# Side work in later slots, in_proj's input two blocks ahead, and three or four parts of the last image under way at once

## The chip, the core and the metric

The kernel runs on one core of one Trainium2 chip. The metric is device time in microseconds (us) from the start of the program to its end; the time of a kernel is the median of its runs. Inside the core five engines have an instruction queue each: TensorE (PE in the profile, with its weight loads as PEld), VectorE (DVE), ScalarE (ACT), GpSimd (POOL) and SyncE (SP), which here only issues DMAs. An engine takes its instructions in order; one that waits for a semaphore holds up all that stand behind it.

## The reference: what is computed

Four images of 64 x 64 positions with 96 channels go through four layers:

- **Layer 0**: a group normalization, then a state-space block: `in_proj` to a value half and a gate half, a depthwise 3x3 convolution with SiLU, and a selective scan in four directions (rows, columns, and both reversed). A step of the scan is `hst = hst * dA + (dl * ul) * B`, the output `y = sum over 16 states of hst * C`. The four directions are merged, normalized, multiplied by the gate and projected back to 96 channels; the input is added.
- **Layer 1**: the same kind of block on the real 2-D Fourier transform of each image (64 x 33 frequencies, 192 channels in), then the inverse transform, added to its input.
- **Layers 2 and 3**: a linear attention over the 4096 tokens of an image (done with a 97 x 97 Gram matrix), and a feed-forward layer of width 384 in fp8 (float8e5), each with a normalization before it and an addition to the token tensor after it.

```
h = h * dA + dt[..., None] * Bt[:, :, None, :] * ut[..., None]
y = jnp.einsum('bkdn,bkn->bkd', h, Ct)
```

## The kernel before, in words

**Three stretches.** The *head* (`begin`, to about 221 us) does the normalization and `project` of the first image pair alone. The *scan loop* (`scans`, L473 to L821) then runs six phases: layer 0 for two image pairs, layer 1 for four images. The *tail* (`end1` of image 3, after 11454 us) finishes the last image alone.

**The scan loop.** It has 1728 steps (L756), one for each segment of up to 512 positions, each quarter of the 16 states and each of three channel chunks. A step is written out in a fixed order (manual schedule, L713), so each engine's queue is exactly the order of the source. VectorE does per step: `hx` scan 0, `hx` scan 1, *slot 1*, `hy` scan 0, *slot 2*, `hy` scan 1, *slot 3*, and the product `hcy` (L781 to L815; the scans' line is L653). TensorE transposes the next step's input (`transposed`, L623) between slots 1 and 2 and accumulates the output (`accumulate`, L675) before and after slot 3. GpSimd forms `hy` (L646) and `hcx` (L798), ScalarE the exponentials (L628) and the scaled inputs `bx` (L593).

**Side work.** All else is cut into pieces by Python generators: a generator yields where its next piece may stand in another slot. `slot` (L733) first lets a piece of the next segment's `prepare` go, then adds `rate / 3` to `due` and takes one side piece when `due` reaches 1:

```
due = min(due + st.z.ph.rate / 3, 3.0)
if due >= 1.0:
    due -= E.step(kind)
```

`RATES` (L26) gives pieces per step for the six phases. A piece marked `LATE` only goes into slot 3, where VectorE's side work is cheap to place; `E.defer(fn)` queues an instruction (a PSUM eviction, an addition) that is issued at the beginning of the next piece, or of the next slot that is held. `E.psum` in the loop hands out one PSUM bank, so a piece's first matmul follows the last reader of the bank. The side tasks of phases 0 to 5 are, in this order: `flip0`, `begin0` of the second pair, two `gate0`; `end0` of a pair and `begin1` of two images (phases 1 and 2); `end1` of images 0, 1, 2 (phases 3, 4, 5). `E.require` (L770) would drain the queue outside the slots if a phase's input were late, and `E.finish` (L821) drains what is left after the last step.

**Places that the change touches.** `visits` (L184): in_proj's input `xi` is loaded one block ahead into two buffers, two yields before the first matmul (L176). `gated` (L350): per block of up to 8 rows, tiles of two rows are loaded (`yt`, `ut`, L364), added up on TensorE (`py`, L394 and L400), and normalized: mean `pm` (L414), subtraction on VectorE (L417), square (L420), variance `pv` (L424), then L431, L436 and the output projection. `out0` (L878) adds the projection `po` to `xr` on VectorE (L901); `out1` (L907) writes `att`. `inverse` (L990): three groups of 32 channels, one after the other: `piv` (L1021), `pio` (L1037), addition (L1040), write. `tokens` (L1049): per layer the eight weight tensors, then `layer_norm` (four parts of 8 tiles, pipelined over its own steps), the Gram matrix `pg` (L1136) and a chain of four small matmuls, eight groups of attention (`pt` L1157, copy `xt` L1159, `pao` L1163, addition L1165), a second `layer_norm`, eight groups of feed-forward (`ptf` L1172, cast `x8` L1174, `ph` L1180, copies L1181, VectorE L1184 and L1187, `pfo` L1192, copy L1200, additions L1202 and L1206), and at the end one store of the whole image (L1207).

In the head and the tail a side task runs alone with 8 PSUM banks and `wide=4`; no manual schedule holds there, and Tile's scheduler orders each queue. In the head, `project` already runs its three chunks through `together`, which takes one piece of each of several generators in turn (L111).

Of the kernel before, what the change touches and what calls it, by code (L numbers as in the profile page):

```python
# [6 lines left out]
F32 = mybir.dt.float32  # L7
# [14 lines left out]
C, P = 3, 128  # L22
# [3 lines left out]
RATES = [1.75, 2.25, 2.35, 2.35, 2.35, 2.35]  # L26
# [97 lines left out]
class Block:  # L124
# [59 lines left out]
    def visits(self, E, sp, wi, xf, blocks, half, nm, w, done):  # L184


        def load(r, n):
            x = sp.tile([CH, 2, 512], F32, name=f"xi{half}_{nm}_{r}", tag=f"xin{w}", bufs=2)
            self.nc.sync.dma_start(out=x[:, :, : n * 64], in_=xf[:, :, r * 64 : (r + n) * 64])
            return x  # L190

        nxt = load(*blocks[0])
        yield
        yield
        for b, (r, n) in enumerate(blocks):
            x, nxt = nxt, load(*blocks[b + 1]) if b + 1 < len(blocks) else None
            pi = E.psum(f"pi{half}_{nm}_{r}")
            yield from self.in_proj(pi, wi, half, x, n * 64)
            E.defer(lambda r=r, n=n, pi=pi: done(r, n, pi))
            yield  # L200
# [149 lines left out]
    def gated(self, E, g, io, out_proj):  # L350


        nc, cfg = self.nc, self.cfg
        yn, yo = io["y"][cfg.nat], io["y"][1 - cfg.nat].rearrange("k (w r) c -> r w k c", r=cfg.NR)
        u, gz = io["u"][cfg.nat], io["gz"]
        with E.pool(f"{cfg.pre}nm{g}") as sp:
# [3 lines left out]
            tiles = [  # L360
                (b, i, r + i, min(2, n - i)) for b, (r, n) in enumerate(cfg.rows) for i in range(0, n, 2)
            ]

            def load(b, i, r, n):  # L364
                nm = f"{cfg.pre}_{g}_{r}"
                yt = sp.tile([P, 2, 2, C * P], F32, name=f"yt_{nm}", tag="yt", bufs=2)
# [5 lines left out]
                ut = sp.tile([P, C, P], F32, name=f"ut_{nm}", tag="ut", bufs=2)  # L372
                nc.sync.dma_start(out=ut[:, :, : n * 64], in_=u[:, :, r * 64 : (r + n) * 64])
                return yt, ut

            todo = iter(tiles)
            nxt = load(*next(todo))
            yield
            yield
            yield  # L380
            for b, (r, nr) in enumerate(cfg.rows):
                n = nr * 64
                nm = f"{cfg.pre}_{g}_{r}"
                z = sp.tile([P, C, 512], F32, name=f"zb_{nm}", tag="zb")
                nc.sync.dma_start(out=z[:, :, :n], in_=gz[:, :, r * 64 : r * 64 + n])
                y = sp.tile([P, C, 512], F32, name=f"yb_{nm}", tag="yb")
                for i in range(0, nr, 2):
                    m = min(2, nr - i) * 64
                    yt, ut = nxt
                    more = next(todo, None)  # L390
                    nxt = load(*more) if more else None
                    ps = E.psum(f"py_{nm}_{i}")[:, : C * P].rearrange("p (c t) -> p c t", c=C)
                    for c in range(C):
                        nc.tensor.matmul(  # L394
                            ps[:, c, :m], self.skip[:, c, :], ut[:, c, :m], start=(c == 0), stop=False
                        )
                    yield
                    for c in range(C):
                        for k in range(4):
                            nc.tensor.matmul(  # L400
                                ps[:, c, :m],
                                yt[:m, k // 2, k % 2, c * P : (c + 1) * P],
                                self.ident[:m, :m],
                                start=False,
                                stop=(c == C - 1 and k == 3),
                                is_transpose=True,
                            )
                        if c < C - 1:
                            yield
                    E.defer(lambda i=i, m=m, ps=ps, y=y: nc.scalar.copy(y[:, :, i * 64 : i * 64 + m], ps[:, :, :m]))  # L410
                    yield
                pm = E.psum(f"pm_{nm}")
                for c in range(C):
                    nc.tensor.matmul(pm[:, :n], self.mean_w, y[:, c, :n], start=(c == 0), stop=(c == C - 1))  # L414
                    yield
                for c in range(C):
                    nc.vector.tensor_tensor(y[:, c, :n], y[:, c, :n], pm[:, :n], ALU.subtract)  # L417
                yield
                sq = sp.tile([P, C, 512], F32, name=f"sq_{nm}", tag="sq")
                nc.scalar.activation(sq[:, :, :n], y[:, :, :n], AF.Square)  # L420
                yield
                pv = E.psum(f"pv_{nm}")
                for c in range(C):
                    nc.tensor.matmul(pv[:, :n], self.mean_w, sq[:, c, :n], start=(c == 0), stop=(c == C - 1))  # L424
                    yield
                ln = sp.tile([P, 512], F32, name=f"ln_{nm}", tag="ln")
                nc.scalar.activation(ln[:, :n], pv[:, :n], AF.Ln, bias=self.eps)
                nc.scalar.activation(pv[:, :n], ln[:, :n], AF.Exp, scale=-0.5)
                yield
                for c in range(C):  # L430
                    nc.vector.scalar_tensor_tensor(  # L431
                        y[:, c, :n], y[:, c, :n], self.lnw[:, c : c + 1], pv[:, :n], ALU.mult, ALU.mult
                    )
                yield LATE
                for c in range(C):
                    nc.vector.scalar_tensor_tensor(  # L436
                        y[:, c, :n], y[:, c, :n], self.lnb[:, c : c + 1], z[:, c, :n], ALU.add, ALU.mult
                    )
                yield
                yield from out_proj(E, sp, wo, y, r, nr)  # L440
# [437 lines left out]
def out0(images, ins, x0):  # L878


    def task(E, blk, sp, wo, y, r, nr):
# [3 lines left out]
        for i, b in enumerate(images):  # L885
# [4 lines left out]
            for m in range(4):  # L890
# [8 lines left out]
                if m % 2:  # L899
                    yield  # L900
            nc.vector.tensor_tensor(xr, xr, po, ALU.add)  # L901
# [5 lines left out]
def out1(att, b):  # L907


    def task(E, blk, sp, wo, y, r, nr):  # L910
        nc = E.nc
        a = sp.tile([HH, 8, 2 * CH], F32, name=f"ab_{b}_{r}", tag="ab")
# [77 lines left out]
def inverse(E, cst, att, x, b, x1):  # L990
# [3 lines left out]
    G, HC, WP = 32, 16, 64  # L994
    xs, xd = (t.rearrange("(h w) c -> w h c", w=WW) for t in (x, x1))
    with E.pool(f"fi{b}") as sp:
# [5 lines left out]
        def load(c0):  # L1002
            a = sp.tile([2 * HH, WP, G], F32, name=f"at_{b}_{c0}", tag="at", bufs=2)
# [7 lines left out]
        nxt = load(0)  # L1011
        yield
        yield
        for c0 in range(0, CH, G):
            a, nxt = nxt, load(c0 + G) if c0 + G < CH else None
            v = sp.tile([2 * WP, G, HH], F32, name=f"v_{b}_{c0}", tag="v")
# [11 lines left out]
            for h0 in range(0, HH, 2 * HC):  # L1028
                xr = sp.tile([2 * WW, HC, G], F32, name=f"xr1_{b}_{c0}_{h0}", tag="xr", bufs=2)
# [11 lines left out]
                for p, h in halves:  # L1041
                    nc.sync.dma_start(out=xd[:, h, c0 : c0 + G], in_=xr[p])
        yield
# [5 lines left out]
def tokens(E, ins, consts, ident, x1, b, out):  # L1049


    nc = E.nc
    A = CH + 1
    with E.pool(f"tk{b}") as sp:
# [3 lines left out]
        nc.sync.dma_start(out=mask, in_=consts["head_mask"])  # L1058
        x = sp.tile([P, NT, CH], F32, name=f"tok_{b}", tag="tok")
        nc.sync.dma_start(out=x, in_=x1.rearrange("(p t) c -> p t c", t=NT))  # L1060
        xn = sp.tile([P, NT, A], F32, name=f"xn_{b}", tag="xn")
        nc.gpsimd.memset(xn[:, :, CH:A], 1.0)
        yield
        yield

        def layer_norm(nm):

            Q = 8
# [8 lines left out]
            for i in range(n + 2):  # L1077
# [3 lines left out]
                if i < n:  # L1081
                    t0 = i * Q
                    s = sp.tile([P, 2, Q], F32, name=f"lns_{nm}_{t0}", tag="lns", bufs=3)
# [13 lines left out]
                if i < n:  # L1097
                    sq = sp.tile([P, Q, CH], F32, name=f"lnq_{nm}_{t0}", tag="lnq", bufs=2)
                    nc.scalar.activation(sq, xq, AF.Square)
# [5 lines left out]

        def small(rows, lhs, rhs, name, into):
# [4 lines left out]

        for ly in (2, 3):
            nm = f"{b}_{ly}"
            wq = sp.tile([A, 3 * CH], F32, name=f"wqkv_{nm}", tag="wqkv")
            nc.sync.dma_start(out=wq, in_=ins[f"l{ly}_wqkv"])
            wqt = sp.tile([CH, A], F32, name=f"wqt_{nm}", tag="wqt")
            nc.sync.dma_start(out=wqt, in_=ins[f"l{ly}_wqt"])
            wff = sp.tile([CH, CH], F32, name=f"wff_{nm}", tag="wff")
            nc.sync.dma_start(out=wff, in_=ins[f"l{ly}_wff"])
            bff = sp.tile([A, CH], F32, name=f"bff_{nm}", tag="bff")  # L1120
            nc.sync.dma_start(out=bff, in_=ins[f"l{ly}_bff"])
            q = {}
            for name, shape in (("w1", [CH, 4 * CH]), ("w2", [P, 3, CH]), ("b1", [P, 3]), ("b2", [P, CH])):
                t = sp.tile(shape, F32, name=f"{name}_{nm}", tag=name)
                src = ins[f"l{ly}_{name}"]
                nc.sync.dma_start(out=t, in_=src.to_broadcast([P, CH]) if name == "b2" else src)
                q[name] = sp.tile(shape, F8, name=f"q{name}_{nm}", tag=f"q{name}")
                yield LATE
# [281 lines left out]
```

## Time and profile before

| what | value |
|---|---|
| median of 3 runs (lowest to highest) | 11915.16 us (11897.1 to 11918.08) |
| the profiled execution, own time | 11917.7 us |
| its span (first to last instruction) | 11915.9 us |
| granted TensorE clock over the span | 0.880 |
| VectorE busy in the loop, 300 to 11455 us | 10230.52 of 11155 us |
| TensorE busy there | 8885.92 us |
| first scan starts, last scan ends | 220.8 us, 11453.6 us |
| last image's gated block, 11458 to 11646 us | TensorE busy 120.52 of 188 us |
| last image's inverse transform, 11646 to 11694 us | TensorE busy 35.10 of 48 us |
| last image's two token layers, to the end | from about 11694 us |

The profiled execution took 11917.7 us, 1.8 us more than its span and 2.5 us more than the median. A row of groups reads: line, engine, operation, tiles, count, busy time, mean duration, and the idle time of that engine just before it with what ended it. A row of waits reads: who waited, for whom, total us, times, longest. A row of stretches gives the busy time of each engine in a window of the span, then the granted TensorE clock (1 is full speed), the DMA engines' mean busy share, and GB/s.

### The profile page before, as it was taken

The page shows a single profiled execution, that of the slowest core. Times are in us where ns is not written, and L with a number is a line of the kernel's source. Part 1 is how long each engine was busy: PE and PEld are TensorE (multiplying, and loading weights), DVE is VectorE, ACT ScalarE, POOL GpSimd, SP SyncE. Part 2 cuts the span into 40 slices and gives each one's busy share as a digit, 9 for nine tenths or more (in the row PEclk, how much of TensorE's full clock was granted, in tenths as well). Part 3 has the DMA queues.
Part 4 walks back from the last instruction along what each step waited for, and adds up shares of the span by engine and source line. Part 5 has one row for each costly group of instructions (what it writes and reads, how often), then busy time and mean ns, then how long its engine had stood idle before and what let it go on. Part 6 is the DMA issues. An engine that isn't in the chain of part 4 may idle for free. (4 is left out here: it accounts for less than half of the span.)

```text
span 11915.9 us, 164932 instructions
## 1 busy us (share of the span) xinstructions
PE 9346.5 (78%) x54800; PEld 6707.9 (56%) x54800; DVE 10559.1 (89%) x10183; ACT 9087.2 (76%) x18534; POOL 8930.4 (75%) x7074
## 2 busy tenths in 40 slices
PE   6678777787788778777888888788778877887765
PEld 3455555555666556556665565565556555565544
DVE  6899999999998999998889988988989899899954
ACT  3678888898777888887768877777777777777733
POOL 2889999888877898987668878877668766686630
PEclk8789989989888989998889989898889888897886
DMA  5454444556555455455543443544234422442231
GB/s 142 119 139 119 121 125 112 141 161 161 148 145 118 124 132 136 126 133 162 149 123 118 132 127 113 155 134 117 82 96 149 112 90 85 143 129 88 83 106 35
DMA packets 1270448, 1469.07 MB, mean 123 GB/s; under 512 B 496024, under 2 KB 1033824, under 8 KB 1260120
## 3 DMA queue, kind: packets, MB, share of 16 engines
q1 hardware_dynamic: 1269591, 1458.53, 44.5%
q8 instruction: 430, 7.05, 0.3%
q14 instruction: 427, 3.49, 0.1%
HBM read 1221.74 MB, written 236.50 MB: 122 GB/s over the span
## 5 line engine op out<-in xcount | busy, mean ns | idle before, releaser
L646 POOL TENSOR_TENSOR hy_l<-du_l,bc_l 128x512 f32<-128x512 f32 (+2 forms) x3456 | 3957.2, 1166 | 2071.9 <-DVE hcy_l L815 1162.3
L798 POOL TENSOR_TENSOR hcx_l<-hx_l,bc_l 128x1024 f32<-128x1024 f32 (+2 forms) x1616 | 3524.4, 2181 | 254.3 <-DVE hx_l L653 218.3
L593 ACT ACTIVATE bx_l<-dut_l,bt_l 128x192 f32<-128x192 f32 (+2 forms) x6272 | 2792.8, 498 | 0.0
L675 PE MATMUL acc_l<-ident,hcx_l 128*128 128x128 f32 (+1 forms) x12000 | 1845.4, 301 | 392.8 <-POOL hcx_l L798 387.7
L628 ACT ACTIVATE ax_l<-delta_l,l_alog 128x512 f32<-128x512 f32 (+2 forms) x3456 | 2139.3, 667 | 0.0
L675 PE MATMUL acc_l<-ident,hcy_l 128*128 128x128 f32 (+1 forms) x11994 | 1830.5, 300 | 349.6 <-DVE hcy_l L815 345.6
L675 PEld LDWEIGHTS acc_l<-ident,hcy_l 128*128 128x128 f32 (+1 forms) x11994 | 1533.7, 154 | 911.2 <-DVE hcy_l L815 523.0
L675 PEld LDWEIGHTS acc_l<-ident,hcx_l 128*128 128x128 f32 (+1 forms) x12000 | 1505.6, 154 | 885.6 <-POOL hcx_l L798 667.9
L815 DVE TENSOR_TENSOR hcy_l<-hy_l,bc_l 128x1024 f32<-128x1024 f32 (+2 forms) x1615 | 1955.2, 1211 | 43.0
L653 DVE TENSOR_TENSOR_SCAN hx_l<-ax_l,state_l,b_l 128x512 f32<-128x512 f32 (+2 forms) x1648 | 1785.8, 1124 | 209.9 <-PE b_l L623 153.8
L653 DVE TENSOR_TENSOR_SCAN hy_l<-b_l,state_l,hy_l 128x512 f32<-128x512 f32 (+2 forms) x1648 | 1782.0, 1119 | 80.5 <-ACT b_l L628 73.3
L628 ACT ACTIVATE b_l<-delta_l,l_alog 128x512 f32<-128x512 f32 (+2 forms) x1912 | 1196.4, 628 | 742.2 <-DVE hx_l L653 707.9
L623 PE MATMUL b_l<-ident,bx_l 128*128 128x128 f32 (+1 forms) x6718 | 1178.2, 303 | 389.7 <-DVE hy_l L653 197.9
L628 ACT ACTIVATE ab_l<-delta_l,l_alog 128x512 f32<-128x512 f32 x1321 | 906.8, 689 | 599.6 <-DVE hx_l L653 550.9
L623 PEld LDWEIGHTS b_l<-ident,bx_l 128*128 128x128 f32 (+1 forms) x6718 | 826.8, 153 | 875.2 <-DVE hy_l L653 320.7
L653 DVE TENSOR_TENSOR_SCAN hx_l<-ax_l,state_l,ab_l 128x512 f32<-128x512 f32 x962 | 1176.8, 1264 | 78.9 <-PE ab_l L623 54.8
L653 DVE TENSOR_TENSOR_SCAN hy_l<-ab_l,state_l,hy_l 128x512 f32<-128x512 f32 x961 | 1172.1, 1257 | 62.7 <-POOL hy_l L646 33.9
L623 PE MATMUL ab_l<-ident,bx_l 128*128 128x128 f32 x5288 | 878.0, 301 | 414.5 <-DVE hy_l L653 227.4
L666 POOL COPY state_l<-hx_l 128x2 f32<-128x2 f32 x1344 | 1140.2, 848 | 0.0
L623 PEld LDWEIGHTS ab_l<-ident,bx_l 128*128 128x128 f32 x5288 | 640.9, 152 | 745.3 <-DVE hy_l L653 339.3
L272 PE MATMUL pc_l<-pad_l,l_dg 128*128 128x512 f32 (+2 forms) x1656 | 791.9, 566 | 69.9 <-ACT uh_l L250 63.9
L176 PE MATMUL pi_l<-xi_l,l_wi 96*128 96x384 f32 (+6 forms) x912 | 466.5, 626 | 246.7 <-DMA xi_l<-xn 94.7
(193 smaller groups left out, 11940.5 us busy)
## 6 DMA issues: line engine op xcount, KB each, us to landing
bc_l<-l_xd_l SPq DMA_DIRECT2D x1536, 256.0 KB
bc_l<-l_xd_l SPq DMA_DIRECT2D x384, 512.0 KB
bc_l<-l_xd_l SPq DMA_DIRECT2D x384, 384.0 KB
us_l<-l_u SPq DMA_DIRECT2D x96, 768.0 KB
l_y<-y_l SPq DMA_DIRECT2D x288, 256.0 KB
bc_l<-l_xd_l SPq DMA_DIRECT2D x192, 320.0 KB
yt_l<-l_y SPq DMA_DIRECT2D x264, 192.0 KB
yt_l<-l_y SPq DMA_DIRECT2D x128, 384.0 KB
```

What stands on the lines that cost most here:

```text
L176: self.nc.tensor.matmul(out[i * cfg.PI : (i + 1) * cfg.PI, :n], wi[:, ki, half, :], xin[:, max(i, ki), :n], start=(ki == 0), stop=(ki == c ...
L272: nc.tensor.matmul(pc[:, : n * 64].rearrange("p (r w) -> p r w", w=64), diag[:, t, :], pad[:, r - p0 + dy : r - p0 + dy + n, dx : dx + 64] ...
L593: nc.scalar.activation(t[:n, b, :, ch], z.dut[:n, b, :, ch], AF.Copy, scale=z.bt[:n, b, m : m + 1])
L623: nc.tensor.transpose(pb[:, t : t + n], st.z.bx[st.q, j][:n, b, st.c], ident[:n, :n])
L628: nc.scalar.activation(out, z.delta[:, st.c, : z.S], AF.Exp, scale=z.blk.A[:, st.c, z.k, n : n + 1])
L646: nc.gpsimd.tensor_tensor(st.hy[:, j, :S], st.z.du[:, st.c, :S], st.z.b[st.q][:, j, :S], ALU.mult)
L653: nc.vector.tensor_tensor_scan(h[:, j, : z.S][:, ::step], a[:, : z.S][:, ::step], b[:, : z.S][:, ::step], 0.0 if z.first else z.state[st.c ...
L666: copy(z.state[st.c][:, n0 : n0 + 2].rearrange("p (j o) -> p j o", o=1), h[:, :, e : e + 1])
L675: nc.tensor.matmul(z.acc[st.c][:n, b, :], hc[:, j, t : t + n], ident, start=(n0 + j == 0 and b == 0), stop=(n0 + j == NST - 1 and b == 0), ...
L798: nc.gpsimd.tensor_tensor(hcx[:, :, :S], hx[:, :, :S], z.c[q][0][:, :, :S], ALU.mult)
L815: nc.vector.tensor_tensor(hcy[:, :, :S], st.hy[:, :, :S], z.c[q][1][:, :, :S], ALU.mult)
```

## The change

- `RATES` goes from `[1.75, 2.25, 2.35, 2.35, 2.35, 2.35]` to `[1.75, 2.35, 2.5, 2.5, 2.5, 2.5]`.
- `visits` loads two blocks ahead into three buffers, and yields three times before the first matmul.
- Additional yields put VectorE's reading of a PSUM bank (or of a ScalarE copy) one slot further on: before L417, L901, the flush of L1165, and L1202.
- `tokens` issues a layer's eight weight loads together, for layer 2 ahead of the load of `x`; the four casts follow later.
- With `wide` above 1 (the tail): `gated` runs three workers, block numbers 0 and 3, 1 and 4, and 2; `inverse` loads all three channel groups and runs them through `together`; `tokens` loads both layers' weights before the inverse transform begins, and runs four parts of 8 tiles each through attention, normalization, feed-forward and the next layer's normalization, with a store for each part.

```diff
-RATES = [1.75, 2.25, 2.35, 2.35, 2.35, 2.35]
+RATES = [1.75, 2.35, 2.5, 2.5, 2.5, 2.5]
...
-            x = sp.tile([CH, 2, 512], F32, name=f"xi{half}_{nm}_{r}", tag=f"xin{w}", bufs=2)
+            x = sp.tile([CH, 2, 512], F32, name=f"xi{half}_{nm}_{r}", tag=f"xin{w}", bufs=3)
...
-        nxt = load(*blocks[0])
+        ahead = [load(*blk) for blk in blocks[:2]]
+        yield
         yield
         yield
         for b, (r, n) in enumerate(blocks):
-            x, nxt = nxt, load(*blocks[b + 1]) if b + 1 < len(blocks) else None
+            ahead += [load(*blk) for blk in blocks[b + 2 : b + 3]]
+            x = ahead.pop(0)
...
+            def worker(w):
+                blocks = list(enumerate(cfg.rows))[w::W]
...
                     for c in range(C):
                         nc.tensor.matmul(pm[:, :n], self.mean_w, y[:, c, :n], start=(c == 0), stop=(c == C - 1))
                         yield
+                    yield
                     for c in range(C):
                         nc.vector.tensor_tensor(y[:, c, :n], y[:, c, :n], pm[:, :n], ALU.subtract)
...
+            yield from together([worker(w) for w in range(W)], W)
...
                 if m % 2:
                     yield
+            yield
             nc.vector.tensor_tensor(xr, xr, po, ALU.add)
...
+        if W > 1:
+            loads = [load(c0) for c0 in range(0, CH, G)]
+            yield from together([channels(w * G, a, w) for w, a in enumerate(loads)], W)
...
+        loads = [weights(ly) for ly in (2, 3)]
+        ws = [next(loads[0])] + ([next(loads[1])] if W > 1 else [])
+        yield
         x = sp.tile([P, NT, CH], F32, name=f"tok_{b}", tag="tok")
         nc.sync.dma_start(out=x, in_=x1.rearrange("(p t) c -> p t c", t=NT))
...
+        def attend(nm, g, w, wo):
...
+            xs = x[:, g * 4 : g * 4 + 4, :]
+            yield
+            E.defer(lambda: nc.vector.tensor_tensor(xs, xs, po, ALU.add))
+            yield
...
+            E.defer(lambda: nc.scalar.copy(y16, po))
+            yield
+            yield LATE
...
+        def part(ly, p, wo, q):
+            nm, w = f"{b}_{ly}", p % W
+            groups = range(p * Q // 4, (p + 1) * Q // 4)
+            for g in groups:
+                yield from attend(nm, g, w, wo)
+            yield from layer_norm(nm + "f", p)
+            for g in groups:
+                yield from feed(nm, g, w, q)
+            if ly == 2:
+                yield from layer_norm(f"{b}_3a", p)
+            else:
+                t = slice(p * Q, (p + 1) * Q)
+                nc.sync.dma_start(out=out[b].rearrange("(p t) c -> p t c", t=NT)[:, t], in_=x[:, t])
...
+            if W > 1:
+                yield from together([part(ly, p, wo, q) for p in parts], W)
+                continue
...
+            rest = tokens(E, ins, consts, ident, x1[b], b, out)
+            if E.wide > 1:
+                yield next(rest)
             yield from inverse(E, consts, att, x0[b], b, x1[b])
-            yield from tokens(E, ins, consts, ident, x1[b], b, out)
+            yield from rest
```

In the loop `wide` is 1: there the bodies of `gated`, `inverse` and `tokens` issue the same instructions as before, with the additional yields and the moved weight loads.

## The prediction

> **What bounds the kernel now.** I read the page's busy shares first, then VectorE's own waits in the scan loop, then busy time and clock by stretch for the tail.
>
> ```profile
> PE 9346.5 (78%) x54800; PEld 6707.9 (56%) x54800; DVE 10559.1 (89%) x10183; ACT 9087.2 (76%) x18534; POOL 8930.4 (75%) x7074
> ...
> DVE  6899999999998999998889988988989899899954
> ```
>
> VectorE is the busiest engine, and its slices stand at 8 or 9 from head to tail. In the loop (300 to 11455 us) it is busy for 10230.52 of 11155 us, so some 925 us of idle VectorE is all that the loop part can win. Its largest waits there:
>
> ```profile
> DVE hx_l L653 <- PE b_l L623: 172.0, 98, 7.8
> DVE hx_l L653 <- PE ab_l L623: 103.7, 42, 7.9
> DVE xr L901 <- PE po L892: 90.3, 30, 9.2
> ...
> DVE tok L1165 <- PE pao L1163: 46.3, 31, 3.9
> ...
> DVE y L1202 <- ACT y L1200: 27.4, 22, 3.7
> DVE qw L1129 <- DMA w<-in_l_w: 26.0, 3, 10.1
> DVE yb_l L417 <- PE pm_l L414: 25.8, 18, 4.0
> ```
>
> The last five of these rows are side work: an addition, subtraction or cast that stands in VectorE's queue before TensorE, ScalarE or a DMA is done with its input, while the next scans wait behind it. They sum to 216 us, and the change moves each of the five. The first two rows are scans that wait for transposes.
>
> The tail (from 11458 us) is another matter: one image alone, engines taking turns.
>
> ```profile
> 11458.00:11487.00 29.00, 14.49 (x72) 13.28 (x72) 0.00 (x0) 1.69 (x4) 0.00 (x0) 0.62 0.82 216
> ...
> 11458.00:11646.00 188.00, 120.52 (x564) 88.22 (x564) 25.47 (x45) 27.76 (x49) 0.00 (x0) 0.80 0.45 114
> 11646.00:11694.00 48.00, 35.10 (x409) 26.08 (x408) 4.14 (x7) 7.35 (x13) 2.86 (x4) 0.89 0.80 99
> ...
> 11731.00:11761.00 30.00, 23.65 (x103) 20.66 (x102) 13.48 (x22) 12.17 (x31) 0.00 (x0) 0.52 0.03 8
> 11761.00:11815.00 54.00, 26.84 (x151) 14.50 (x150) 38.86 (x72) 31.98 (x86) 0.00 (x0) 0.50 0.00 0
> ```
>
> Columns are PE, PEld, DVE, ACT, POOL busy, then granted clock, DMA share, GB/s. The gated block leaves TensorE idle for 67 of 188 us; attention is TensorE at half clock; feed-forward has no engine above 72%.
>
> **The loop, part by part.** One slot further on is about two scans of 1.2 us (rows of L653), 2.4 us. Cutting every single wait at 2.4 us, what goes is 51 of 90 us at L901, 43 of 46 at L1165, 21 of 26 at L417 and 22 of 27 at L1202; what is longer than 2.4 us stays. The weight loads of L1129 are now issued before `x` and several slots before the cast: all 26 us. Sum 163 us.
>
> The additional yields need slots: from the yields, `end0` takes 277 instead of 253, `begin1` 278 instead of 272, `end1` 453 instead of 415. The rates rise by 4.4% and 6.4%, so in `end0` and `end1` the density of real work stays as it was, and in `begin1` it rises by 2 to 4%. No phase has to drain its queue early; four pieces of the last `end1` are left after the last step. Cost: nothing in the loop, as long as TensorE (8885.92 of 11155 us) has room.
>
> Two blocks ahead: scans that wait while TensorE has stood before L176 for `xi` in the 9 us ahead of it make up 71 of the first two rows' 276 us (36 in `begin0`, 34 in `begin1` and its gate). L176 itself waits 49.3 us for `xi<-xn` in 8 cases and 60.3 us for `xi<-xf` in 22. These are mostly first blocks of a part; the third yield gives them one piece more, 1/1.75 of a step of about 6.7 us = 3.8 us in phase 0, against waits of 4 to 8 us. I take half, 35 us.
>
> Of 163 + 35 = 198 us not all comes back: a stall of VectorE is also time in which TensorE and GpSimd catch up, and the next in line is `hx` behind L623. In the stretches with L901 TensorE is 80 to 90% busy. I take 70%: **140 us**. Bounds: 0 (all of it becomes waits for L623) to 287 us (216 + 71, all of it gone).
>
> **The head.** In_proj of the first chunk's second part waits 3.6 and 2.2 us for `xi` at 139 and 144 us, because SP stands before the store of `uh` ahead of its loads; in the changed order one more of them is issued before that store. TensorE runs without a gap from there to the convolution's end. **5 us**, 0 to 10.
>
> **The tail**, by the changed program's order on each engine:
>
> - *Gated*: 11 tiles of 960 KB and three `zb` (13 MB) now come in one go. At the 216 GB/s of the first stretch they take 60 us, where TensorE would need 11 x 2.9 = 32. Then `pm`, `pv` and `po` of three blocks (2.9, 4.3 and 10.3 us for 8 rows) with the chain's pauses covered, about 40; the second round of 6 and 5 rows about 50; start 4. And the four left pieces put the previous image's 1.5 MB store ahead of these loads: 7. Sum 161 for 188: 27 won; 10 to 50.
> - *Inverse*: 17 weight loads and the mask stand in SP's queue ahead of the reads of `att`. Before, eight such loads kept SP from 11697.8 to 11709.3 us; here I take 9 us, plus 5 because all three groups' reads must land before the lockstep moves on, less 2 of pauses: **12 lost**; 0 to 20.
> - *First normalization*: the wait for weights goes (the reductions began at 11703.9 us, the subtraction at 11711.9), but the four parts move in lockstep: some 8 us of all parts' reductions and subtractions (0.95 us each) stand ahead of the first variance, and ScalarE's 32 scalings (2.23 us for 8) with the small ones, 12 us, come after it. From `x` landed to the end of `pg`, 24.3 us become about 20: 4 won.
> - *Attention, twice*: eight groups took 29 us with TensorE waiting 0.7 us for each copy. In lockstep TensorE never waits: 8 x (1.0 + 2.0) = 24 us at this clock: 10 won.
> - *Feed-forward with its normalization, twice*: 54 us before. After: 10 us to the first transpose, ScalarE's scalings ahead of the `ph` copies, then two rounds of four groups with VectorE the bound at 3.8 us a group; 48 us each: 12 won.
> - *Normalization between the layers*: before it was pipelined under the feed-forward; from the last `pfo` to the end of `pg` went 9 us. In the new order all four parts' reductions follow the last addition: 8 + 12 + 1.5 = 21.5. **13 lost.**
> - *Store in four*: 3 won.
>
> Sum 27 - 12 + 4 + 10 + 12 - 13 + 3 = 31 us. The clock is the open term. In the loop, at 0.88, the same attention matmuls (8685 to 8725 us) have a mean of 290 and 306 ns; in the tail, at 0.52, 433 and 400. Were the lockstep's TensorE granted that clock, 24 us would be about 16, 16 us more for both layers. I take a third: **36 us** in all. Bounds: -10 to 90.
>
> [...]
>
> **Sum.** 140 + 5 + 36 = 181 us off the profiled execution's 11917.7 us gives 11736.7; that execution lies 2.5 us above the median, so 11734, say **11735 us**.
>
> **The rivals.**
>
> 1. *The waits only move.* VectorE leaves a slot earlier and meets the same late TensorE at L623. For it: the two L623 rows are the largest, and at 3600 to 3700 us TensorE is busy for 95 of 100 us while VectorE has 76. Against: such stretches are short, and the five waits lie mostly elsewhere. The loop wins nothing; 11917.7 - 41 - 2.5 = 11874 us.
> 2. *The tail wins nothing* (clock stays, lockstep exposes what was pipelined, the loads collide): 11770 us.
> 3. *All goes*: 287 + 5 + 60 = 352 us: 11563 us.
> 4. *Slower: denser side work starves TensorE in `begin1`* (3650 to 5405 and 6110 to 7680 us, some 3300 us).
>
> ```profile
> 3600.00:3700.00 100.00, 95.17 (x739) 84.40 (x740) 76.09 (x64) 65.33 (x140) 66.68 (x49) 0.73 0.58 102
> 3800.00:3900.00 100.00, 82.70 (x486) 58.24 (x487) 98.88 (x82) 86.22 (x181) 90.57 (x66) 0.97 0.41 111
> ```
>
> Where TensorE is full, its clock is 0.73 and VectorE loses 23 us in 100. If 2 to 4% more pieces tipped more stretches into that state, each 100 us would cost 23. To undo the 181 us and lose 24 more, 890 us of the 3300 would have to tip; at 1000 us the time is 11965. Against it: TensorE is at 80 to 83% there, and 4% of its side share is 1 to 2 points.
>
> **Chances.** Forecast 53%, rival 1 17% (12% faster, 5% within 0.2%), rival 2 15%, rival 3 8%, rival 4 7%. 0.2% is 24 us, about what a measurement of this kernel tells from no change: faster 88%, same 5%, slower 7%. The range of 11620 to 11885 us leaves out rivals 3 and 4 and the part of rival 1 that lies within 0.2%: 20%.
>
> **What would show it.** VectorE's waits at the lines of L901, L1165, L417, L1202 and L1129 should fall from 216 to about 55 us, with the two rows behind L623 rising by no more than 60; a rise as large as the fall is rival 1. `xi` should vanish from most of TensorE's waits. The tail should take some 425 us instead of 460, attention about 16 to 24 us for a layer; a clock of 0.5 there is the lower end. VectorE's share falling below 80% in more than the Fourier stretches is rival 4. I am wrong if the loop's length (11233 us from first to last scan) changes by less than 70 or more than 250 us.

## The result, and the profile after

The changed kernel takes **11707.02 us** (median of 4 runs, 11697.82 to 11716.54) against 11906.49 us of the kernel before, measured beside it on the same chip: a ratio of 0.9832, 95% interval 0.9815 to 0.9849. Its profiled execution took 11706.21 us, with a span of 11704.4 us. In the two profiles the 211.5 us between the spans lie so: the head 5.3 us (the first scan starts at 215.5 instead of 220.8 us), the loop 140.0 us (first to last scan 11092.8 instead of 11232.8 us), the tail 66.2 us (396.1 instead of 462.3 us).

The page after, the same rows as before:

```profile
PE 9301.7 (79%) x54800; PEld 6722.3 (57%) x54800; DVE 10549.4 (90%) x10183; ACT 9089.0 (78%) x18533; POOL 8931.5 (76%) x7075
...
DVE  6899999999999998999888989988999999899974
```

VectorE's busy time is nearly that of before (10559.1 us); the span has become shorter around it. VectorE's waits in the loop (who waited, for whom, total us, times, longest):

```profile
DVE hx_l L660 <- PE b_l L630: 168.9, 111, 10.0
DVE hy_l L660 <- ACT b_l L635: 101.2, 94, 9.7
DVE hx_l L660 <- PE ab_l L630: 97.3, 42, 8.9
DVE hy_l L660 <- ACT ab_l L635: 49.7, 47, 4.2
...
DVE xr L909 <- PE po L899: 21.6, 14, 3.8
...
DVE y L1230 <- ACT y L1227: 10.9, 21, 1.6
DVE tok L1193 <- PE pao L1190: 9.3, 12, 2.6
...
DVE yb_l L421 <- PE pm_l L417: 1.2, 3, 0.5
DVE qw L1095 <- DMA w<-in_l_w: 1.1, 1, 1.1
```

The five moved waits (the last five rows) fell from 216 to 44 us. The scans' waits for TensorE (rows 1 and 3) fell slightly, from 276 to 266 us, while those of the second scans for ScalarE (rows 2 and 4) rose from 126 to 151 us. Now the tail by stretch (PE, PEld, DVE, ACT, POOL busy; granted clock, DMA share, GB/s): gated block, inverse transform, first attention, first feed-forward, the normalization between the layers with its Gram matrix.

```profile
11316.00:11461.00 145.00, 104.84 (x564) 82.97 (x564) 25.11 (x46) 26.84 (x48) 0.00 (x0) 0.84 0.65 155
11461.00:11527.00 66.00, 36.67 (x408) 26.37 (x408) 5.92 (x19) 7.51 (x13) 2.73 (x4) 0.74 0.63 88
11564.00:11575.00 11.00, 10.68 (x97) 10.51 (x96) 5.18 (x10) 4.09 (x8) 0.00 (x0) 1.00 0.00 0
11575.00:11619.00 44.00, 24.90 (x152) 15.27 (x152) 36.41 (x71) 28.87 (x76) 0.00 (x0) 0.65 0.00 1
11619.00:11642.00 23.00, 10.24 (x64) 9.36 (x64) 11.62 (x19) 13.34 (x45) 0.00 (x0) 0.55 0.00 0
```

Row 3 is the surprise: attention runs at the full clock, TensorE busy for 10.68 of 11 us, where it had 0.52 in 30 us before.

### The profile page after: what moved, and what is told of

It is laid out like the page before. It is cut to its first block, busy times and chain, and to the rows that moved or that the text cites. A ratio compares the mean times of both kernels' runs of the same rounds, so it can differ in the third digit from the quotient of the medians.

```text
span 11704.4 us, 164864 instructions
## 1 busy us (share of the span) xinstructions
PE 9301.7 (79%) x54800; PEld 6722.3 (57%) x54800; DVE 10549.4 (90%) x10183; ACT 9089.0 (78%) x18533; POOL 8931.5 (76%) x7075
## 5 line engine op out<-in xcount | busy, mean ns | idle before, releaser
L682 PE MATMUL acc_l<-ident,hcx_l 128*128 128x128 f32 (+1 forms) x12006 | 1876.0, 305 | 392.6 <-POOL hcx_l L805 388.4
L660 DVE TENSOR_TENSOR_SCAN hx_l<-ax_l,state_l,ab_l 128x512 f32<-128x512 f32 x962 | 1176.5, 1263 | 49.3 <-PE ab_l L630 27.3
L274 PE MATMUL pc_l<-pad_l,l_dg 128*128 128x512 f32 (+2 forms) x1656 | 787.9, 564 | 56.0 <-ACT uh_l L252 46.6
```

What stands on the lines that cost most here:

```text
L274: nc.tensor.matmul(pc[:, : n * 64].rearrange("p (r w) -> p r w", w=64), diag[:, t, :], pad[:, r - p0 + dy : r - p0 + dy + n, dx : dx + 64] ...
L660: nc.vector.tensor_tensor_scan(h[:, j, : z.S][:, ::step], a[:, : z.S][:, ::step], b[:, : z.S][:, ::step], 0.0 if z.first else z.state[st.c ...
L682: nc.tensor.matmul(z.acc[st.c][:n, b, :], hc[:, j, t : t + n], ident, start=(n0 + j == 0 and b == 0), stop=(n0 + j == NST - 1 and b == 0), ...
```

## The experiments

Times below are medians; since the kernel before had medians of 11905.6 to 11918.9 us on the four chips of these runs, parts are compared by their ratio to it, run beside them, times 11906 us; each such ratio has a 95% interval of some 18 us either way. Loop and tail lengths are of the profiled executions, one of each kernel. Eight kernels with the same code in the tail (after, e1, e2, e3, e7, e9, e10, e12) took 386.6 to 403.6 us for it, so some 10 us there are scatter. e1 to e12 are the kernels of the numbers below.

**1 to 3: the parts.** The later slots (with RATES) and in_proj's second block are undone, one, the other, or both.

```diff
-            x = sp.tile([CH, 2, 512], F32, name=f"xi{half}_{nm}_{r}", tag=f"xin{w}", bufs=3)
+            x = sp.tile([CH, 2, 512], F32, name=f"xi{half}_{nm}_{r}", tag=f"xin{w}", bufs=2)
...
-        ahead = [load(*blk) for blk in blocks[:2]]
-        yield
+        ahead = [load(*blk) for blk in blocks[:1]]
...
-            ahead += [load(*blk) for blk in blocks[b + 2 : b + 3]]
+            ahead += [load(*blk) for blk in blocks[b + 1 : b + 2]]
```

```diff
-RATES = [1.75, 2.35, 2.5, 2.5, 2.5, 2.5]
+RATES = [1.75, 2.25, 2.35, 2.35, 2.35, 2.35]
...
-                    yield
+                    if E.wide > 1:
+                        yield
                     for c in range(C):
                         nc.vector.tensor_tensor(y[:, c, :n], y[:, c, :n], pm[:, :n], ALU.subtract)
...
-            yield
             nc.vector.tensor_tensor(xr, xr, po, ALU.add)
...
-            yield
+            if W > 1:
+                yield
             E.defer(lambda: nc.vector.tensor_tensor(xs, xs, po, ALU.add))
...
-            yield
+            if W > 1:
+                yield
             yield LATE
```

The first diff is e2, the second e3, both together e1.

> The kernel after with the later slots, the new RATES and in_proj's second block ahead all undone: what is left of the change is the tail with its parts, and the eight weight loads issued together ahead of x in the loop. My theory (the prediction's terms): the loop wins only the 26 us of weight waits, of which 70% come back, 18 us, and the tail keeps the 66 us that the trace of after shows: 11906 - 18 - 66 = about 11822 us. Rival: a cast that no longer waits only lets the next wait come earlier, or the freed queue changes nothing, so the loop stays as before: about 11840 us. Below 11800 us would say that the later slots and the second block bring less than the loop's 140 us, and something else in the loop brings the rest.

> The kernel after with in_proj's input one block ahead in two buffers and two yields again; all else as in after. The prediction gives this part 35 us of stall at 70%, 25 us, and the head 5 us: 11707 + 30 = 11737 us. Rival, from the result: phase 0 holds none of the five moved waits and keeps its rate, and yet became 34 us shorter; so the second block ahead brings that, and about as much again in the phases with begin1: 11707 + 5 + 34 + 20 to 34 = 11766 to 11780 us. The waits of the scans for TensorE in phase 0 should come back from 15 to some 40 us under both.

> The kernel after with the four additional yields undone in the loop (kept in the tail) and the old RATES; the second block ahead, the weight loads and the tail as in after. By the prediction this part holds 137 us of the five waits, 70% of it time: 11707 + 96 = 11803 us, with the four rows of waits (the addition to xr, the addition to the tokens, the addition of b2's copy, the subtraction of the mean) back at some 190 us. Rival, the waits only move to the scans' waits for TensorE: the time rises by less than 40 us, to at most 11747 us. If the second block ahead brings more than I gave it, this part brings less, and the time is 11780 us.

| undone | us | ratio, 95% | loop | so the part is worth |
|---|---|---|---|---|
| nothing (after) | 11707.0 | 0.9832 (0.9815 to 0.9849) | 11092.8 | |
| both (e1) | 11824.6 | 0.9931 (0.9916 to 0.9946) | 11213.7 | left: 82 us by ratio; its loop is 19 us shorter than before's, its tail 71 |
| second block (e2) | 11760.7 | 0.9876 (0.9860 to 0.9891) | 11155.4 | 52 us by ratio, 63 by loop |
| slots and RATES (e3) | 11776.2 | 0.9890 (0.9875 to 0.9905) | 11168.5 | 69 us by ratio, 76 by loop |

The parts add up: 82 + 52 + 69 = 203 us, against 200. e1 came out where my theory had it (11822 us). No run undoes the weight loads alone: their share is what e1's loop keeps, 19 us, with VectorE's wait for `w` at 1.8 us instead of 26.0. By their middle values e2 says that I gave the second block half of its worth, e3 that I gave the slots a third too much; with intervals of 18 us the times alone do not settle either, the traces below say more. Where the slots' gain went is in VectorE's waits of e3:

```profile
DVE hx_l L661 <- PE b_l L631: 125.1, 86, 8.3
DVE xr L909 <- PE po L900: 109.2, 29, 9.1
DVE hx_l L661 <- PE ab_l L631: 105.4, 44, 9.9
DVE hy_l L661 <- ACT b_l L636: 83.7, 89, 4.2
DVE tok L1194 <- PE pao L1190: 46.2, 31, 3.6
DVE hy_l L661 <- ACT ab_l L636: 42.7, 39, 3.7
```

From e3 to after the four slot waits fall from 196 (109.2 + 46.2 + 24.2 + 16.0) to 43 us, by 153. In return the scans wait longer for TensorE (230.5 to 266.2) and for ScalarE (126.4 to 150.9): 60 us return as other waits, as the first rival said, but not all.

**4: density alone**, the kernel before with the new RATES.

```diff
-RATES = [1.75, 2.25, 2.35, 2.35, 2.35, 2.35]
+RATES = [1.75, 2.35, 2.5, 2.5, 2.5, 2.5]
```

> The kernel before with nothing changed but the new RATES (2.25 to 2.35 and 2.35 to 2.5 pieces a step from phase 1 on), so that side work is really denser by 4 to 6% there and its queue runs empty earlier. The forecast's theory (TensorE has room): within 20 us of before, 11906 us. The fourth rival (denser side work starves TensorE where it is nearly full): phases 1 and 2 alone, 4077 us, become 1 to 2.5% longer, 11950 us or more, with the wait of the scans for TensorE above 330 us instead of 276.

Measured 11952.5 us, ratio 1.0039 (1.0025 to 1.0053): slower, as the rival had it. Phase 2 (from its first scan to the next phase's) took 1538 us instead of 1479. The named mechanism is only partly there: over the loop the two rows of scans behind TensorE sum to 266 us, 276 before (the 330 expected did not come). In phase 2 VectorE's waits are these:

```profile
DVE xr L901 <- PE po L892: 63.1, 15, 7.7
DVE hx_l L653 <- PE ab_l L623: 52.8, 22, 6.9
DVE hx_l L653 <- PE b_l L623: 26.3, 20, 7.0
```

Before they were 46.6, 37.3 and 24.2 us: TensorE is late for all its readers there. Part of the 59 us is work done earlier: phase 2 has 7759 matmuls instead of 7306, and phase 5 is 40 us shorter. What remains over the whole is the 47 us. So my term "cost: nothing in the loop" does not hold for the rates by themselves.

**5: the tail's weight loads on ScalarE's queue.**

```diff
-                nc.sync.dma_start(out=t, in_=src.to_broadcast([P, CH]) if name == "b2" else src)
+                (nc.scalar if W > 1 else nc.sync).dma_start(
+                    out=t, in_=src.to_broadcast([P, CH]) if name == "b2" else src
+                )
```

> The kernel after with the 16 weight loads of the tail (and only of the tail) issued from ScalarE's queue instead of SP's; ScalarE has nothing to do between the last copy of the gated block and the first copy of the inverse transform. In the trace of after SP issues these loads and the mask for 18.7 us (11462 to 11481 us) before it comes to the reads of att, and the inverse transform's first matmul stands at 11495, 33 us after the last projection, where it was 9.6 us before. My theory: SP's queue is what delays it; the reads of att are issued at 11462 and the tail becomes 14 to 18 us shorter: 11707 - 16 = about 11691 us. Rival: the reads of att wait for the att writes or for each other anyway (three groups' reads, 1.6 MB): the first matmul moves by less than 5 us, 11703 us or more.

Measured 11711.2 us, ratio 0.9835 (0.9819 to 0.9852), tail 397.0 us: nothing won. (The first inverse matmul of after stands at 11487; 11495, in the expectation, is the third group's.) After, then e5: SP's six reads of `att`, and the inverse matmuls of the third group on.

```profile
11480.76 9.49 SPq L1015 DMA_DIRECT2D at<-att  x6
11494.68 5.58 PE L1026 MATMUL piv<-ih,at 128*64 128x64 f32 x86 [1.51 <-DMA at<-att]
```

```profile
11470.55 20.31 SPq L1015 DMA_DIRECT2D at<-att  x6
11495.48 4.72 PE L1026 MATMUL piv<-ih,at 128*64 128x64 f32 x72 [1.65 <-DMA at<-att]
```

Counted from the last projection (11461.0 us in after, 11464.0 in e5), the reads begin 13 us earlier, but their issue takes 11 us longer, and the third group arrives only 2 us earlier. What holds them up are SP's own waits in e5 (11464 to 11492 us; after has none at that line):

```profile
SPq L1015 <- DMA wqt<-in_l_wqt: 7.8, 1, 7.8
SPq L1015 <- DMA bff<-in_l_bff: 4.5, 1, 4.5
```

Two of the reads are issued only when a weight load of ScalarE's queue has landed, 12.3 us in all; in the trace each of them waits for the semaphore that this load updates. The theory that SP's order alone delays the inverse transform falls. Whether the transfers also slowed each other no run here shows.

**6: attention group by group again, in the tail.**

```diff
-            for g in groups:
-                yield from attend(nm, g, w, wo)
             yield from layer_norm(nm + "f", p)
...
             if W > 1:
+                for g in range(NT // 4):
+                    yield from attend(nm, g, g % 2, wo)
                 yield from together([part(ly, p, wo, q) for p in parts], W)
```

> The kernel after with the tail's attention groups one after the other again (transposes, copy, matmuls, next group), everything else as in after; the normalization's four parts follow. In after the attention takes 10.6 us a layer at a granted clock of 1.00, in before 28 us at 0.53, with a pause of 0.7 us in each of eight groups. Theory: the unbroken lockstep is what gets the full clock. Then the pauses bring back 0.53 and matmuls of 400 to 433 ns, and both layers lose 17 us: 11707 + 35 = about 11742 us. Rival: the clock comes from what went before (the Gram matrix, the denser gated block and inverse), and only the pauses themselves come back, 8 x 0.7 us a layer: 11707 + 11 = about 11718 us, with matmuls of some 275 ns.

```profile
11564.00:11592.00 28.00, 22.44 (x98) 19.81 (x97) 12.02 (x19) 11.20 (x28) 0.00 (x0) 0.51 0.00 1
```

Measured 11738.4 us, ratio 0.9861 (0.9844 to 0.9879), as the theory had it. The same Gram matrix precedes it, the same 96 matmuls take 28 instead of 11 us, at 0.51 instead of 1.00 and a median of 421 instead of 275 ns (`pao`). But the unbroken run does not gain the clock, it keeps it. The attention begins at 11563.9 us in both kernels; ahead of it the clock is 1.00 in both, granted during the Gram matrix. After, then e6 (the end of the Gram matrix with the four small matmuls and e6's first transposes, then the attention):

```profile
11558.20:11564.00 5.80, 4.47 (x43) 3.81 (x43) 0.25 (x1) 0.82 (x4) 0.00 (x0) 1.00 0.00 0
```

```profile
11557.90:11564.60 6.70, 5.23 (x49) 4.36 (x47) 0.51 (x2) 1.33 (x6) 0.00 (x0) 1.00 0.00 0
11564.70:11592.00 27.30, 21.98 (x93) 19.56 (x94) 11.76 (x18) 11.00 (x28) 0.00 (x0) 0.50 0.00 1
```

In before it is the same: 1.00 from 11722.3 to 11732.4 us, 0.50 from there on, with the attention starting at 11731.0. Over all traces, both layers of the nine kernels with unbroken attention have 1.00, both layers of the five with pauses or other work in it (before, e4, e6, e8, e11) 0.51 to 0.55. Of some 17 us that a layer's attention loses, 7.4 come back, since the following normalization now runs partly beneath it: the tail is 417.8 us, 21.7 longer (the medians say 31, the ratios 35; the profiled execution is the fastest of its four). In after the clock goes to 1.00 during the Gram matrix (0.50 from 11540.0 to 11558.1 us, 1.00 from 11558.2 us on); what brings it there is not isolated by any run here. In e6 it goes to 0.50 with TensorE busy for 5.23 of the 6.70 us ahead, and behind that, with TensorE busy for 21.98 of 27.30 us (a pause of 0.7 us in each group), it did not come back. What length of pause the clock bears no run shows.

**7 and 9: fewer pieces in phase 2, more behind it.**

```diff
-RATES = [1.75, 2.35, 2.5, 2.5, 2.5, 2.5]
+RATES = [1.75, 2.35, 2.35, 2.55, 2.55, 2.55]
```

In e9 the line is `RATES = [1.75, 2.35, 2.2, 2.6, 2.6, 2.6]`.

> The kernel after with RATES of 1.75, 2.35, 2.35, 2.55, 2.55, 2.55: fewer pieces a step in phase 2, where begin1 keeps TensorE full, and more in the phases of end1, the same number of pieces in all. The run with the new RATES alone cost 47 us, most of it in phase 2. If that density also costs in after (where the additional yields eat most of it; by count the real work in phase 2 is 1.8% denser than before), phase 2 becomes some 20 us shorter and the whole 10 to 20 us: about 11692 us. Rival: the additional yields already made up for the rates; begin1 only runs on into phase 3, and the time stays within 10 us of 11707.

> The kernel after with RATES of 1.75, 2.35, 2.2, 2.6, 2.6, 2.6: twice the shift of the run with 2.35 and 2.55, which was 23 us faster than after (phase 2 47 us shorter, phases 3 and 4 together 30 us longer). Theory: what counts is the density where TensorE is full; a second shift of the same size takes as much again off phase 2 only while TensorE is still short there, so less: 5 to 20 us, 11664 to 11679 us. Rival: in phase 2 nothing is left to win, begin1 runs on into phase 3 and makes that the full one: 11684 us or more.

e7: **11684.1 us**, ratio 0.9815 (0.9800 to 0.9830). e9: **11681.5 us**, 0.9811 (0.9795 to 0.9828). By their middle values both lie some 20 us below after, but the intervals overlap with after's (0.9815 to 0.9849), and e9 is not told from e7. Phase 2 went from 1470 to 1423 and 1408 us; phases 3 to 5 gave back 26 and 20. Four kernels with the same loop (after, e5, e6, e8) have 1470, 1480, 1480 and 1495 us in phase 2, so some 25 us there are chance, and 47 are more than that. VectorE's largest waits in phase 2 of e7, for the 46.9 and 39.9 us that after has in these rows:

```profile
DVE hx_l L660 <- PE ab_l L630: 29.4, 12, 5.1
DVE hx_l L660 <- PE b_l L630: 25.3, 27, 3.1
```

**8: the parts staggered.**

```diff
             groups = range(p * Q // 4, (p + 1) * Q // 4)
+            for _ in range(4 * p):
+                yield
```

> The kernel after with part p of the tail's token layers started 4 x p pieces later, so that the four parts are no longer in lockstep: while one part normalizes on VectorE and ScalarE, another has matmuls. In after TensorE stands still for the normalization before the feed-forward (8 us a layer) and between the layers (some 10 us from the last matmul to the first of the Gram matrix). Theory: lockstep exposes them, as the prediction's 13 us lost have it; the staggered parts win 10 to 25 us: about 11690 us. Rival: TensorE falls back to half clock when its work is no longer in one piece, which costs the attention up to 17 us a layer: 11720 us or more.

Measured 11710.9 us, ratio 0.9839 (0.9823 to 0.9855); tail 402.7 us, 6.6 longer, which is within the scatter of the tail. Both theories were at work: from the last `pfo` to the first Gram matmul no time is left (10.8 us in after), but attention is at half clock again, below for the second layer. What one gives, the other takes.

```profile
11658.50:11676.00 17.50, 14.01 (x64) 12.42 (x65) 6.52 (x11) 5.78 (x15) 0.00 (x0) 0.55 0.00 1
```

**10: a slot more behind `py`'s eviction**, with RATES 1.75, 2.45, 2.45, 2.65, 2.65, 2.65.

```diff
                         E.defer(lambda i=i, m=m, ps=ps, y=y: nc.scalar.copy(y[:, :, i * 64 : i * 64 + m], ps[:, :, :m]))
                         yield
+                        if W == 1:
+                            yield
```

> The kernel after with one yield more behind each tile of the gated block in the loop, so that the next tile's first matmul (py) stands a slot behind the copy that frees its bank, and RATES of 1.75, 2.45, 2.45, 2.65, 2.65, 2.65 to hold the density of the run with 2.35 and 2.55. In after TensorE waits 80 us for that copy (55 times). The second block ahead took about 70 us of TensorE's waits away and was worth 54 us. Theory: a wait of TensorE is worth its length wherever it stands: 11684 - 50 = about 11634 us. Rival: these waits are short ones (1.5 us each where those for xi were 3 to 5) that the transposes and scans ride over, and the time stays within 10 us of 11684.

Measured 11705.1 us, ratio 0.9830 (0.9814 to 0.9846), 18 us above e7. TensorE's wait behind that copy fell from 67.1 us in e7 (80 in after) to 4.5 us, and the scans' waits for TensorE (179.4 and 97.6 us, in e7 166.6 and 83.9) did not fall: 63 us of TensorE's idle time, in pieces of 1.3 us, went without a gain in time. But phase 2 has the rate 2.45 here, not 2.35, and is 29 us longer, while phases 3 to 5 are 31 us shorter; the two effects are not separated, so that such waits are worth nothing is not shown.

**11: the kernel before with the shift of e7.**

```diff
-RATES = [1.75, 2.25, 2.35, 2.35, 2.35, 2.35]
+RATES = [1.75, 2.25, 2.2, 2.4, 2.4, 2.4]
```

> The kernel before with nothing changed but RATES of 1.75, 2.25, 2.2, 2.4, 2.4, 2.4: fewer pieces a step in phase 2 and as many more behind it. Theory (density costs in phase 2 whatever the kernel): phase 2, 1479 us in before and 1538 with 2.35, becomes some 40 us shorter and the whole 15 to 25 us: about 11886 us. Rival: the price of density begins only above the old rates, and the time stays within 10 us of 11906.

Measured 11932.6 us, ratio 1.0016 (1.0007 to 1.0026); phase 2 1477 us as before, phase 5 25 us longer. The theory that fewer pieces in phase 2 always help falls: it held from 2.5 to 2.35 in both kernels, and below that not in the kernel before. Why, and what lengthens phase 5, stays open.

**12: two blocks ahead, but two yields.**

```diff
         ahead = [load(*blk) for blk in blocks[:2]]
         yield
         yield
-        yield
```

> The kernel after with the third yield before in_proj's first matmul taken out; two blocks are still loaded ahead into three buffers. With the second block and the third yield both undone the time was 11761 us, 54 us above after. The prediction read the waits for xi as those of first blocks, for which only the third yield gives time. By it the waits for xi return to some 100 us from 34, and the time to 11750 us or more. Rival: it is the second block ahead (SP may issue the load a whole block earlier, past stores that hold it) that removes them: the waits stay near 34 us and the time within 10 us of 11707.

Measured 11720.9 us, ratio 0.9833 (0.9817 to 0.9850): by ratio no different from after, by the profile's loop 21 us longer. TensorE's waits for `xi` in e2, e12 and after:

```profile
PE pi_l L176 <- DMA xi_l<-xf: 53.8, 17, 10.0
PE pi_l L176 <- DMA xi_l<-xn: 48.2, 8, 9.0
```

```profile
PE pi_l L176 <- DMA xi_l<-xf: 37.3, 7, 10.8
PE pi_l L176 <- DMA xi_l<-xn: 19.2, 3, 8.7
```

```profile
PE pi_l L176 <- DMA xi_l<-xf: 21.1, 8, 4.5
PE pi_l L176 <- DMA xi_l<-xn: 13.2, 2, 8.7
```

102 us become 56 by the second block and 34 by the third yield. The time follows the first step, not measurably the second; that is close to the rival (waits of 56 us for its 34, 14 us of time for its 10).

## Why the prediction came out as it did

The forecast of 11735 us was 28 us too high, well inside its range, and its case (the loop wins most of it, the tail a little) is what happened. The loop's 140 us were met exactly, but by errors that cancel.

- **The moved waits, 163 us to go.** Right: 172 went, 44 are left (55 predicted), and the rows behind L623 did not rise above before.
- **70% of it comes back (as time won).** Too high for the slots: of 153 us of waits that fell, 69 to 76 became time, about half; 137 x 0.7 = 96 was expected. 60 us returned as waits of scans. For the weight loads 19 us of e1's loop stand against the expected 18.
- **Half of `xi`'s 71 us.** This is the step that failed: 52 to 63 us for 25 in the loop (35 at 70%). I took the waits for those of first blocks. In the trace of before, five of the eight waits for `xi<-xn`, 33.1 of 49.3 us, fall on a block in the middle of a part, 8 matmuls after its first. One of them, with SP's queue:

```profile
1043.42 6.96 SPq L500 DMA_DIRECT2D us_l<-l_u  x1
...
1050.47 3.97 SPq L573 DMA_DIRECT2D bc_l<-l_xd_l  x6
...
1054.54 2.81 SPq L189 DMA_DIRECT2D xi_l<-xn  x2
...
1064.31 1.73 PE L176 MATMUL pi_l<-xi_l,l_wi 96*64 96x448 f32 x2 [6.55 <-DMA xi_l<-xn]
```

  The load of `xi` stands in SP's queue behind a load that waits for its buffer and six broadcasts; issued at 1054.5, it lands at 1064.3. With one block more ahead such a delay is covered: all nine waits of over 0.7 us that after has are first blocks. Nor does 70% hold here: phase 0, where these five waits of 5.5 to 7.6 us lie, is 2586.3 us in before, 2584.9 in e2 and 2551.8 in after, 33 us shorter for 33.1 us of waits. In e12, where the five are gone too, phase 0 is 2560.3 us: 25 us shorter than in e2 for 29 us of waits for `xi<-xn`. So nearly all of these waits became time. That this is because they are longer than the scans in flight can bridge is my reading, not shown by a run.
- **The density costs nothing.** Phase 2 did not become longer (1470 to 1495 us, 1479 before), since the yields eat most of the rates. But it costs something there: with 2.35 instead of 2.5 phase 2 takes 1423 us (e7), some 20 us of which remain over the whole. By itself the same rise costs 47 us (e4), and the fourth rival's price was no fancy.
- **Head, 5 us.** Measured 5.3. The kernels with one block ahead start their first scan at 216.9 to 221.5 us, those with two at 212.4 to 215.8: the difference holds, with a scatter nearly as large as itself.
- **The tail, 36 us.** Measured 66.2, by terms (predicted): gated block 39.8 (27), of the 192.5 us from the last scan to the last `po`; inverse and weights 19.1 lost (12 lost), to the last `pio`; from there to the end of the Gram matrix 1.1 (4); attention with the small matmuls twice 17.4 and 17.5 (10 in all, and a third of 16 for the clock); feed-forward with its normalization 12.8 and 10.1 (12 in all); between the layers 15.4 lost (13 lost); store 2.0 (3). Against the sum, attention won 20 us more, the gated block 13 and the feed-forward 11; the inverse lost 7 more, and the rest 6.

  *Attention.* The clock was not a third but all, and the step from clock to time was mis-sized too: I scaled 24 us by the mean durations (290 and 306 ns to 433 and 400), which gives 16, and 275 to 421 ns would give the same. Measured are 10.8 us. These durations overlap: in after the 96 last 26.3 us in sum and start 0.11 us apart; in e6 they start 0.21 us apart at 421 ns (the busy time per matmul, 10.68 us for 97 against 22.44 for 98, says it too). So the time went with the clock, the durations did not.

  *Gated block.* From the last `py` of the first round to its last `po` it took 35 us (about 40), the second round 44 (about 50).

  *Feed-forward.* 43 us, not 48; its clock is 0.65 where it was 0.50, but no run separates that from the order.

  *Inverse.* 26.1 us pass from the last `po` to the first inverse matmul, 9.7 before: 16 lost where I had 9. SP issues the loads and the mask for 18.7 us ahead of the reads; I had given 17 loads (they are 16) less than the 11.5 us that eight took before. The lockstep itself cost 3 us, as expected (39.8 instead of 37.1 us from the first inverse matmul to the last `pio`). That another queue does not win the 16 us back is what e5 showed.
- **Rival 1** (the waits only move) was true for some 40% of the slots' part and for none of the rest; **rival 2** was wrong by the clock, the gated block and the feed-forward; **rival 3** did not come; **rival 4** showed in full only when its cover, the yields, was taken away.

## What to carry to other kernels

When an engine waits for a DMA, ask of each wait which instance it is (first block or middle) and what stands ahead of that load in the issuing queue: a long queue is beaten by issuing a block earlier, and here nearly all of the waits of 5 to 8 us became time, while 63 us in waits of 1.3 us went with no gain that could be seen (in a run whose rates differed too). Moving a reader one slot back turned about half of the wait it removed into time, the rest returned behind the next producers; and adding slots without work needs a higher rate, whose price must be measured without the slots to be seen. Work that is put side by side so that TensorE is never idle can keep the full clock (1.00 in after) where short pauses lose it (0.51 in e6, with 0.7 us in each group): of the 17 us won per attention layer, the pauses were some 5.5 and the clock the rest, and any staggering that hides another engine's work must be weighed against it. And the time of a run of matmuls is estimated from start to start (0.11 us in after), not from their durations (275 ns there), which overlap.

## What the runs showed of the hardware

- In after the granted clock of the tail's attention stays at 1.00, which it has since the Gram matrix; its 96 matmuls (16 transposes, 32 matmuls, twice) follow each other without a gap, 10.68 of 11 us busy. With a pause of 0.7 us in each group of 12 (e6, busy for 22.44 of 28 us) it is 0.51 over the attention, and with other work between (e8, 14.01 of 17.50 us) 0.55. In e6 it falls to 0.50 at 11564.7 us; the attention began at 11563.9. Transposes of 128x97 take 273 ns in after and 418 in e6 (medians).
- From e6 (0.51) to after (1.00) the `pao` matmuls' duration falls from 421 to 275 ns, their distance from start to start from 0.21 to 0.11 us.
- With sixteen small weight loads moved to ScalarE's queue (e5), SP issued the six reads of `att` in 20.3 us instead of 9.5, and 12.3 us of it were waits for two of these loads to land.
- In before VectorE waited 9.21 us for `po` ahead of the addition to `xr` at 5604.55 us; the product and the scans that stand behind it in VectorE's queue began at 5605.02 and 5605.89 us.
- Phase 2 of one and the same loop took 1470 to 1495 us in four executions (after, e5, e6, e8).
